# Row maxima subtracted once in four key steps, convolution weights loaded late, and GpSimd's product behind the additions

## The chip, the cores and the metric

The kernel runs on one core of a Trainium2 chip. The metric is the device time of one execution in microseconds. A core has five engines that matter here: TensorE (PE; its weight loads are shown apart as PEld), VectorE (DVE), ScalarE (ACT), GpSimd (POOL) and SyncE (SP), which only issues DMAs. Each works through its own list of instructions in order, and waits for the others by semaphores. TensorE writes to PSUM; the other data lie in SBUF.

## What is computed

Two layers, one behind the other, on an input of 2 x 256 x 64 x 64 in float32, so 4096 positions with 256 channels for each of two batches. The first is self-attention with 8 heads of 32 channels, the second a non-local block with 2x2 max pooling. Cut to what matters:

```python
# layer 0, for each batch b and head h; i, j run over 4096 positions
q, k, v = split(w_qkv @ x)
scores = einsum('bhdi,bhdj->bhij', q, k) / sqrt(32)
attn = softmax(scores, axis=-1)
out = einsum('bhij,bhdj->bhdi', attn, v)
x1 = w_proj @ out + x

# layer 1
g_x = maxpool2(conv1x1(x1, g_w, g_b))
theta_x = conv1x1(x1[:, :64], theta_w, theta_b)
phi_x = maxpool2(conv1x1(x1[:, 64:], phi_w, phi_b))
y = softmax(theta_x^T @ phi_x, axis=-1) @ g_x
return batchnorm(conv1x1(y, W_w, W_b)) + x1
```

The softmax subtracts the exact maximum of every row before the exponential, so the maxima of all 4096 x 4096 scores of each head are found first.

## The kernel before

**Quads and blocks.** Four heads are worked on together, one on each group of 32 partitions; that is a quad. Two batches of two quads make four, numbered n = 0 to 3. A quad's 4096 queries come in 8 blocks of 512 (index i), so there are 32 blocks, numbered here 0 to 31 in order of time; the first batch has blocks 0 to 15, the last quad has blocks 24 to 31. A block goes through its keys in 32 steps of 128 keys (index j).

**One step.** `attend` (from L376) issues a step so: `subtract` writes minus the row maxima into a PSUM tile of two banks, one for each head of a pair of heads (L413, a matmul of ones with rows that hold each maximum as a sum of three bfloat16 terms); `score` adds the scores (L401); ACT takes the exponential (L537) into p. A quad is two such pairs, with two tiles. While this goes on, `weigh` for the step before multiplies the exponentials by v (L425), and VectorE adds the result to num (L436).

**Differences of keys.** The subtraction isn't done in every step. An even step subtracts and then adds the scores with its keys. An odd step goes on with the same tile: its keys are taken 512 positions further on, and what is added to the tile are the scores with the differences of the keys of two chunks of 512 (kd for the first half of the positions, last_kd for the second). So the tile holds the odd step's scores less the maxima, with no subtraction. GpSimd makes these differences (L214 in the first quad, `differences` at L229 later).

**Maxima, one block ahead.** In each step, twice, `advance(maxes)` puts in a piece of the search for the next block's maxima: two products of 128 queries with 512 keys each time (L252), on the two groups of 32 rows that the scores beside them don't use. VectorE reduces them, either plainly (L264) or as a pair of chunks: ACT keeps the positive part of the product with a key difference (L271), and VectorE adds the other product and takes the maximum in one instruction (L278). The first block of a new quad has fewer pairs and more plain maxima. At the end of a block's maxima, near step 28, `negate` (L133) splits them in three bfloat16 terms on GpSimd, in one of two tiles by turns, and `make_rows` turns them by four small matmuls (L147) into the rows that `subtract` uses.

**Sums of exponentials.** The denominators are built in part by GpSimd: for two heads it adds each step's p to a running sum (L455), and for the other two it issues a DMA that adds two steps' p to one of two sums (L463, 1 MB each). p comes from rings: 6 buffers for the first kind and 5 double ones for the second, and a buffer is free when its addition or its DMA has ended.

**Normalization** (`normalize`, L465) runs inside the next block. A last accumulating DMA joins the two sums (L469), matmuls make den (L481), ACT copies it to r (L489). SP stores one row of each head and loads it back spread over 128 partitions (L498, L499), VectorE takes the reciprocals there (L503), SP stores them and loads them back broadcast (L504, and four loads at L506), and GpSimd multiplies num by r into y (L511). In the built order L511 stands behind the addition of step 13; nothing in the source ties it there.

**Projections for the blocks to come.** `during` (L233) lists for each block what is made of x: in six of eight blocks, k and v of the next quad together behind step 15, and q of this quad two blocks on behind step 27; in the last two, three items behind steps 11, 19 and 27. `make` (L165) loads x through SP into the single buffer of the pool xs, unless the same part of x is still held there, and does the matmuls (L183, L195). In the last quad there is no next quad, so only q is left.

**Around it.** A prologue of about 103 us makes the first quad's q, k, v and the first maxima. After a batch's 16 blocks, `project` (L557) adds the projected output to x, and `non_local` (L581) does the second layer. The weights of both (wproj, theta, phi) lie in SBUF for the whole run; ACT's queue loads them at the start.

Of the kernel before, what the change touches and what calls it, by code (L numbers as in the profile page):

```python
# [9 lines left out]
F32 = mybir.dt.float32  # L10
BF16 = mybir.dt.bfloat16
# [5 lines left out]
N = HH * WW  # L17
# [18 lines left out]
def conv_attention(  # L36
# [45 lines left out]

    wqk_sb = const.tile([P, NC, QUADS, 2, P], F32, name="wqk_sb")
    wv_sb = const.tile([P, NC, C], F32, name="wv_sb")
    wproj_sb = const.tile([P, NC, C], F32, name="wproj_sb")
    theta_w = const.tile([CM, 2 * CM], F32, name="theta_w")
    phi_w = const.tile([P, NC, 2 * CM], F32, name="phi_w")
    par = const.tile([P, NPAR], F32, name="par")

    def load_x(b, i, t):  # L90
# [7 lines left out]
    nc.scalar.dma_start(out=wproj_sb, in_=wproj.rearrange("(o p) m -> p o m", p=P))  # L98
    nc.scalar.dma_start(out=theta_w, in_=thetaw)
    nc.scalar.dma_start(out=par, in_=params)  # L100

    nc.scalar.dma_start(out=phi_w[CM:P, 0, :], in_=phiw[0 : P - CM, :])
    nc.scalar.dma_start(out=phi_w[:, 1, :], in_=phiw[P - CM :, :])

    ident = work.tile([P, P], F32, tag="r", name="ident", bufs=1)
    make_identity(nc, ident)
# [19 lines left out]

    terms = [const.tile([P, NB // P, QH, D], BF16, name=f"terms_{i}") for i in range(2)]
    for t in terms:  # L130
        nc.gpsimd.memset(t, 0.0)

    def negate(name, n, neg):  # L133


        t = terms[n % 2]
# [28 lines left out]
    def make(what, n, i):  # L165
        b, qd = QUAD[n]
        if (b, i) not in held:
            name = f"x_{what}_{n}_{i}"
            if attending:
                held.clear()  # L170
                to = xs.tile([P, NC, NB], F32, tag="x", name=name)
            else:
                to = single(name)
            held[b, i] = load_x(b, i, to)
        xc = held[b, i]
        name = f"{what}_{b}_{qd}_{i}"
        pq = scratch(name)
        if what == "v":
            if i == 0:
                v[n] = qkv.tile([P, NJ, QH, D], F32, tag="v", name=f"v_{n}")  # L180
            for j in range(NB // P):
                for c in range(NC):
                    nc.tensor.matmul(  # L183
                        pq[:, bass.ts(j, P)],
                        xc[:, c, bass.ts(j, P)],
                        wv_sb[:, c, bass.ts(qd, P)],
                        start=(c == 0),
                        stop=(c == NC - 1),
                    )
                if j % 2 == 1:  # L190
                    yield
            nc.scalar.copy(v[n][:, bass.ts(i, NB // P)].rearrange("p j h d -> p (j h d)"), pq)
            return
        for c in range(NC):
            nc.tensor.matmul(  # L195
                pq,
                wqk_sb[:, c, qd, 0 if what == "q" else 1, :],
                xc[:, c, :],
                start=(c == 0),
                stop=(c == NC - 1),  # L200
            )
            yield
        if what == "q":
            to = q[n, i] = qkv.tile([P, NB], F32, tag="q", name=f"q_{n}_{i}", bufs=3)
        else:
            if i == 0:
                k[n] = qkv.tile([P, N], F32, tag="k", name=f"k_{n}")
            to = k[n][:, bass.ts(i, NB)]
        nc.scalar.copy(to, pq)
        if what == "k" and i % 2 == 1 and n == 0:  # L210
            if i == 1:
                kd[n] = qkv.tile([P, NI // 4, NB], F32, tag="kd", name=f"kd_{n}")
            two = k[n][:, bass.ts(i // 2, 2 * NB)]
# [15 lines left out]
        nc.gpsimd.tensor_sub(to, two[:, :, 1, :], two[:, :, 0, :])  # L229

    def during(n, i):  # L233
        if i < NI - 2:
            return [[("k", n + 1, i), ("v", n + 1, i)], [("q", n, i + 2)]]
        if i == NI - 2:
            return [[("k", n + 1, i)], [("k", n + 1, i + 1)], [("q", n + 1, 0)]]
        return [[("v", n + 1, i - 1)], [("v", n + 1, i)], [("q", n + 1, 1)]]


    reduced, cut = None, None
# [92 lines left out]
    def maxima(n, i):  # L334
        if (n, i) == (0, 0):
            yield from first_block()
        else:
            heads = [of_head(n, i, h) for h in range(QH)]
            for step in range(G * NI):

                for two in ((2, 3) if step % 2 == 0 else (3, 2)), (0, 1):
                    for h in two:
                        next(heads[h])
                    yield
        neg = work.tile([P, NB // P, QH], F32, tag="neg", name=f"neg_{n}_{i}")
        nc.vector.tensor_reduce(neg, part, AX.X, ALU.max, negate=True)
        rows.append(negate(f"{n}_{i}", len(rows), neg))
        if i == 0 and n > 0:
            nc.vector.memset(part[:, :, 2:, :], LEAST)

# [10 lines left out]
    def advance(steps, n=1):  # L361
        for _ in range(n):
            next(steps, None)
# [12 lines left out]
    def attend(b, y):  # L376
# [10 lines left out]

        def keys(j):


            return j // 8 * 8 + j % 2 * 4 + j % 8 // 2

        def score(s, pair, blk, j):

            if j % 2:
                kj = (last_kd if j >= NJ // 2 else kd[blk.n])[:, j // 8 % 2, bass.ts(j % 8 // 2, P)]
            else:
                kj = k[blk.n][:, bass.ts(keys(j), P)]
            for t in range(2):
                h = 2 * pair + t  # L400
                nc.tensor.matmul(  # L401
                    s[:, t, :],
                    kj[bass.ts(h, D), :],
                    q[blk.n, blk.i][bass.ts(h, D), :],
                    start=False,
                    stop=True,
                    skip_group_check=j % 2 == 1,
                )

        def subtract(s, pair, blk):  # L410
# [54 lines left out]
        def normalize(blk):  # L465
# [27 lines left out]
            else:  # L493
# [14 lines left out]
                    )  # L508
                for _ in range(13):
                    yield  # L510
            nc.gpsimd.tensor_mul(y[:, blk.qd, bass.ts(blk.i, NB)], blk.num, r)  # L511

        waiting, normal = None, iter(())
        for qd in range(QUADS):
            for i in range(NI):
                blk = Block(qd, i)
                groups = during(blk.n, i)
                items = [[x for x in g if x[1] < len(QUAD)] for g in groups]
# [38 lines left out]
    def project(b, y, normal):  # L557
        for i in range(NI):
            if i == NI // 2:
                for _ in normal:  # L560
# [17 lines left out]
        return ap.rearrange("p (r a w b) -> p r w a b", a=2, w=WW // 2, b=2)  # L578


    def non_local(b, y):  # L581
# [76 lines left out]
        def maxima1():  # L658
            for i in range(NI):
# [17 lines left out]
                ready.append(negate(f"l1_{b}_{i}", i, neg))  # L677
                yield

        maxes1 = maxima1()  # L680
# [100 lines left out]
    attending = True  # L781
    for b in range(B):
        y = big.tile([P, NC, N], F32, tag="y", name=f"y{b}")
        project(b, y, attend(b, y))
        non_local(b, y)


_OUT = (B, C, HH, WW)
# [51 lines left out]
```

## Time and profile before

Three runs took 4070.07 to 4077.61 us, median 4073.38.

| | us |
|---|---|
| median of three runs | 4073.38 |
| the profiled execution, its own time | 4072.18 |
| its span, from the first instruction to the last | 4070.4 |
| prologue | 0 to 103 |
| attention, batch 0, blocks 0 to 15 | 103 to 1809 |
| projection and second layer, batch 0 | 1809 to 2100 |
| attention, batch 1, blocks 16 to 31 | 2100 to 3777 |
| projection and second layer, batch 1 | 3777 to 4070 |

The attention is 3383 of the 4070 us. How busy each engine is there shows in the view by windows. Its columns are the stretch, its length, and for each engine its busy time and number of instructions, then the granted clock, DMA's share and GB/s:

```profile
103.00:954.00 851.00, 849.73 (x6972) 316.45 (x6968) 678.92 (x1284) 635.62 (x790) 688.60 (x408) 1.00 0.77 160
2952.00:3777.00 825.00, 812.12 (x6542) 280.39 (x6539) 625.15 (x1159) 617.66 (x754) 650.19 (x390) 0.99 0.77 161
```

The order is PE, PEld, VectorE, ACT, POOL. The first line is quad 0, the second quad 3, which makes no k and v. In both PE is busy almost throughout, at the full clock, and VectorE, ACT and POOL for 75 to 81% of the time.

A matmul of float32 operands is recorded as two matmuls. That is why L425, with four matmuls in a step, shows as a group of 8. The subtraction's operands are bfloat16, and there the record is one.

### The profile page before, as it was taken

What the parts mean: (1) busy time and instruction counts of PE and PEld (TensorE: products, weight loads), DVE (VectorE), ACT (ScalarE), POOL (GpSimd) and SP (SyncE); (2) the same over time, 40 slices, a digit from 0 to 9 for tenths busy, and PEclk for the clock granted to TensorE, in tenths of its full rate; (3) what the DMA queues carried; (4) which work ended last, traced back from release to release, by engine and by line L of the source; (5) the groups of instructions that cost most, each with busy time, mean ns of one, the idle gap of its engine ahead of it and who ended that gap; (6) DMA issues with size and microseconds to landing.
All of it is one profiled execution on the core that took longest, in us unless ns stands there. A gap on an engine that the chain in (4) does not pass through costs nothing.

```text
span 4070.4 us, 75211 instructions
## 1 busy us (share of the span) xinstructions
PE 4021.6 (99%) x29616; PEld 1495.2 (37%) x29616; DVE 2974.8 (73%) x5451; ACT 2673.8 (66%) x3329; POOL 2892.5 (71%) x1844
## 2 busy tenths in 40 slices
PE   9999999999999999999999999999999999999998
PEld 4333333333333333333333333333333333332333
DVE  5877877788778777774457777777888888784444
ACT  5777777777777777751147777777677777776111
POOL 0888887778778888761457888787888888776143
PEclk9999999999999999999999999999999999999999
DMA  1677777777777777780027777778777777778200
GB/s 59 143 161 161 155 164 160 159 162 164 156 161 163 165 161 160 165 197 0 25 51 159 161 161 162 165 160 173 161 165 161 158 155 164 154 151 173 76 16 26
DMA packets 113380, 569.35 MB, mean 140 GB/s; under 512 B 20232, under 2 KB 22024, under 8 KB 51840
## 3 DMA queue, kind: packets, MB, share of 16 engines
q0 software_dynamic: 68832, 501.25, 60.5%
q1 hardware_dynamic: 42928, 62.10, 5.0%
q8 instruction: 232, 3.80, 0.4%
q10 hardware_dynamic: 1264, 1.19, 0.1%
q14 instruction: 124, 1.02, 0.1%
HBM read 54.39 MB, written 8.88 MB: 16 GB/s over the span
## 4 chain that ended last, share of the span: by engine, by line
PE 89%; DMA 5%; DVE 2%; POOL 1%; issue 1%; ACT 1%; SPq 0%; POOLq 0%; DVEq 0%; ACTq 0%
PE ps L252 27%; PE w L425 23%; PE s L401 17%; PE y L698 5%; PE s L413 5%; DMA p<-p 3%; DMA flat<-few 2%; PE q L195 2%; PE den L481 1%; PE k L195 1%; PE proj L567 1%; PE g L623 1%; PE v L183 1%; DVE r L712 1%; PE f L666 1%
## 5 line engine op out<-in xcount | busy, mean ns | idle before, releaser
L455 POOL TENSOR_TENSOR p<-p,p 128x1024 f32<-128x1024 f32 x945 | 2331.0, 2467 | 444.5 <-ACT p L537 308.1
L252 PE MATMUL ps<-k,q 32*128 32x512 f32 x6232 | 2116.6, 618 | 2.4 <-DVE part L278 1.0
L537 ACT ACTIVATE p<-s 128x1024 f32<-128x1024 f32 x2048 | 1987.3, 1026 | 134.2 <-PE ps L252 46.1
L264 DVE TENSOR_REDUCE part<-ps 128x1 f32<-128x512 f32 x2136 | 1372.6, 686 | 138.2 <-PE s L401 66.4
L425 PE MATMUL w<-p,v 128*32 128x512 f32 x8192 | 1093.4, 605 | 0.0
L278 DVE CUSTOM_DVE_ANT_0 ps<-ps,over 128x512 f32<-128x512 f32 x980 | 683.8, 700 | 540.3 <-PE ps L252 299.1
L401 PE MATMUL s<-q,k 32*128 32x512 f32 x4096 | 1038.0, 594 | 0.0
L271 ACT ACTIVATE over<-ps 128x512 f32<-128x512 f32 x916 | 546.9, 597 | 578.2 <-PE ps L252 533.9
L252 PEld LDWEIGHTS ps<-k,q 32*128 32x128 f32 x6232 | 788.8, 184 | 261.6 <-DVE num L436 75.4
L436 DVE TENSOR_TENSOR num<-num,w 128x512 f32<-128x512 f32 x992 | 671.7, 677 | 42.3 <-PE w L425 39.4
L252 PE MATMUL ps<-kd,q 32*128 32x512 f32 x1056 | 568.4, 643 | 1.0 <-POOL kd L214 0.7
L401 PE MATMUL s<-q,last_kd 32*128 32x512 f32 x2048 | 515.2, 616 | 12.1 <-ACT p L537 12.1
L401 PE MATMUL s<-q,kd 32*128 32x512 f32 x2048 | 513.1, 617 | 2.0 <-ACT p L537 2.0
L252 PE MATMUL ps<-last_kd,q 32*128 32x512 f32 x904 | 482.1, 640 | 1.5 <-POOL last_kd L214 1.5
L425 PEld LDWEIGHTS w<-p,v 128*32 128x32 f32 x8192 | 161.5, 108 | 778.9 <-ACT over L271 689.4
L463 POOL DMA_DIRECT2D p<-p x448 | 388.4, 867 | 70.7 <-ACT p L537 67.4
L413 PE MATMUL s<-rows,ones_b 32*128 32x512 bf16 x2048 | 394.5, 381 | 0.1
L401 PEld LDWEIGHTS s<-q,k 32*128 32x128 f32 x4096 | 371.3, 184 | 10.6 <-issue 7.2
L413 PEld LDWEIGHTS <-ones_b 32*128 32x128 bf16 x2048 | 132.6, 91 | 504.4 <-PE ps L252 251.6
L401 PEld LDWEIGHTS s<-q,last_kd 32*128 32x128 f32 x2048 | 172.5, 184 | 232.4 <-ACT p L537 219.9
L401 PEld LDWEIGHTS s<-q,kd 32*128 32x128 f32 x2048 | 174.8, 185 | 224.4 <-ACT p L537 196.8
L698 PE MATMUL y<-p,kv 128*128 128x512 f32 x512 | 240.0, 608 | 6.4 <-DVE r L712 6.4
(106 smaller groups left out, 2239.7 us busy)
## 6 DMA issues: line engine op xcount, KB each, us to landing
p<-p POOLq DMA_DIRECT2D x478, 1024.0 KB, 7.6
x_k<-in_x_dram SPq DMA_DIRECT2D x32, 512.0 KB
x_q<-in_x_dram SPq DMA_DIRECT2D x30, 512.0 KB
x_res<-in_x_dram SPq DMA_DIRECT2D x16, 512.0 KB
out_dram<-z SPq DMA_DIRECT2D x16, 512.0 KB
r<-flat SPq DMA_DIRECT2D x120, 64.0 KB
x_v<-in_x_dram SPq DMA_DIRECT2D x6, 512.0 KB
wqk_sb<-in_wqk_dram ACTq DMA_DIRECT2D x1, 512.0 KB
```

Source lines behind the costliest of these rows:

```text
L252: nc.tensor.matmul(ps, q[n, i][bass.ts(h, D), bass.ts(g, P)], keys[bass.ts(h, D), :], start=True, stop=True,)
L264: reduced = nc.vector.tensor_reduce(part[:, g, h, j : j + 1], ps, AX.X, ALU.max)
L271: cut = nc.scalar.activation(over, ps, AF.Relu)
L278: reduced = nc.vector.tensor_tensor_reduce(out=ps, in0=ps, in1=over, scale=1.0, scalar=LEAST, op0=ALU.add, op1=ALU.max, accum_out=part[:, ...
L401: nc.tensor.matmul(s[:, t, :], kj[bass.ts(h, D), :], q[blk.n, blk.i][bass.ts(h, D), :], start=False, stop=True, skip_group_check=j % 2 == 1,)
L413: nc.tensor.matmul(s[:, t, :], ones_b[bass.ts(h, D), :], rows[blk.rows][bass.ts(h, D), :], start=True, stop=False,)
L425: nc.tensor.matmul(w[bass.ts(h, D), :], v[blk.n][:, keys(j), h, :], p[h // 2][:, h % 2, :], start=True, stop=True,)
L436: nc.vector.tensor_add(blk.num, blk.num, w)
L455: added = nc.gpsimd.tensor_add(blk.sums[0], blk.sums[0], p[0])
L463: nc.gpsimd.dma_start(out=blk.sums[n], in_=two, accum_op=ALU.add)
L537: nc.scalar.activation(p[pair], s, AF.Exp, scale=scale)
L698: nc.tensor.matmul(acc[i][o], wg[:, 2 * t + j, bass.ts(o, P)], p[:, j, :], **edge)
```

## The change

**Keys in fours.** A half of the positions (2048) has four chunks of 512. Steps now go through them in fours: the first with the keys of chunk 0, the next with kd (chunk 1 less chunk 0), then with a new tile mid_kd (chunk 2 less chunk 1), then with the second part of kd or last_kd (chunk 3 less chunk 2). `subtract` is called, and a tile taken, in one step of four instead of one of two. mid_kd is a constant tile of two halves that GpSimd fills in the new function `between`: in the prologue for the first quad, later in step 18 of the block before a quad (first half) and in step 2 of a quad's first block (second half).

**Weights.** The three weights leave the constant tiles. `late_weights` takes the buffer of x at the end of a batch's attention and loads them there by four DMAs of SP, once for each batch.

**One tile of terms** instead of two.

**Order of the projections.** All blocks now have up to three items behind steps 11, 19 and 27: q first, then k, then v, where k and v were together before.

**The product with the reciprocals** is issued behind `added`, the last addition that stands before it in the source. In the built order that is step 25's addition.

Two effects show in the built order of SP: the load of x for k stands before the store of the reciprocals (L504) in most blocks, and the weights' loads stand before those of x_res. The instructions of VectorE are the same, in the same order.

```diff
-    wproj_sb = const.tile([P, NC, C], F32, name="wproj_sb")
-    theta_w = const.tile([CM, 2 * CM], F32, name="theta_w")
-    phi_w = const.tile([P, NC, 2 * CM], F32, name="phi_w")
...
+    def late_weights(b):
+
+        t = xs.tile([P, NC, NB], F32, tag="x", name=f"weights_{b}")
+        project_w = t[:, 0, :].rearrange("p (c m) -> p c m", c=NC)
+        phi_w = t[:, 1, :C].rearrange("p (c m) -> p c m", c=NC)
+        theta_w = t[:CM, 1, C : C + 2 * CM]
+        nc.sync.dma_start(out=project_w, in_=wproj.rearrange("(o p) m -> p o m", p=P))
+        nc.sync.dma_start(out=theta_w, in_=thetaw)
+
+        nc.sync.dma_start(out=phi_w[CM:P, 0, :], in_=phiw[0 : P - CM, :])
+        nc.sync.dma_start(out=phi_w[:, 1, :], in_=phiw[P - CM :, :])
+        return project_w, theta_w, phi_w
...
-    terms = [const.tile([P, NB // P, QH, D], BF16, name=f"terms_{i}") for i in range(2)]
-    for t in terms:
-        nc.gpsimd.memset(t, 0.0)
...
+    t = const.tile([P, NB // P, QH, D], BF16, name="terms")
+    nc.gpsimd.memset(t, 0.0)
...
+        if what == "k" and i % 4 == 2 and n == 0:
+            between(n, i // 4)
...
+    mid_kd = const.tile([P, 2, NB], F32, name="mid_kd")
+
+    def between(n, half):
+        two = k[n][:, N // 2 * half + NB :]
+        nc.gpsimd.tensor_sub(mid_kd[:, half, :], two[:, NB : 2 * NB], two[:, :NB])
...
         if i < NI - 2:
-            return [[("k", n + 1, i), ("v", n + 1, i)], [("q", n, i + 2)]]
+            return [("q", n, i + 2), ("k", n + 1, i), ("v", n + 1, i)]
...
-            return j // 8 * 8 + j % 2 * 4 + j % 8 // 2
+            return j // 16 * 16 + j % 4 * 4 + j % 16 // 4
 
         def score(s, pair, blk, j):
 
-            if j % 2:
-                kj = (last_kd if j >= NJ // 2 else kd[blk.n])[:, j // 8 % 2, bass.ts(j % 8 // 2, P)]
+            half, c, cols = j // 16, j % 4, bass.ts(j % 16 // 4, P)
+            if c == 0:
+                kj = k[blk.n][:, bass.ts(keys(j), P)]
+            elif c == 2:
+                kj = mid_kd[:, half, cols]
             else:
-                kj = k[blk.n][:, bass.ts(keys(j), P)]
+                kj = (last_kd if half else kd[blk.n])[:, c // 2, cols]
...
-            nc.gpsimd.tensor_mul(y[:, blk.qd, bass.ts(blk.i, NB)], blk.num, r)
+            with tc.issue_after(added.ins):
+                nc.gpsimd.tensor_mul(y[:, blk.qd, bass.ts(blk.i, NB)], blk.num, r)
...
-                        if j % 2 == 0:
+                        if j % 4 == 0:
                             s = both[pair] = scores(f"s_{blk.name}_{j}_{pair}")
                             subtract(s, pair, blk)
                             advance(maxes)
...
+                        if (i, j) == (0, 2) and blk.n > 0:
+                            between(blk.n, 1)
                         if (i, j) == (0, NJ // 4) and blk.n > 0:
                             differences(blk.n, 1, last_kd)
-                    elif items and j in ((15, 27), (11, 19, 27))[len(groups) - 2]:
-                        for item in items.pop(0):
-                            advance(make(*item), 9)
+                        if (i, j) == (NI - 1, NJ // 2 + 2) and blk.n + 1 < len(QUAD):
+                            between(blk.n + 1, 0)
+                    elif j % 8 == 3 and j > 8 and items:
+                        advance(make(*items.pop(0)), 9)
```

More of the change, by code (lines that the diff above doesn't have):

```diff
@@ L97, in conv_attention @@
     nc.scalar.dma_start(out=wv_sb, in_=wv.rearrange("(o p) m -> p o m", p=P))
-    nc.scalar.dma_start(out=wproj_sb, in_=wproj.rearrange("(o p) m -> p o m", p=P))
-    nc.scalar.dma_start(out=theta_w, in_=thetaw)
     nc.scalar.dma_start(out=par, in_=params)
-    nc.scalar.dma_start(out=phi_w[CM:P, 0, :], in_=phiw[0 : P - CM, :])
-    nc.scalar.dma_start(out=phi_w[:, 1, :], in_=phiw[P - CM :, :])
+    def late_weights(b):
[8 more added lines that the diff above has]
+        return project_w, theta_w, phi_w
     ident = work.tile([P, P], F32, tag="r", name="ident", bufs=1)
@@ L124, in conv_attention, with negate @@
     nc.vector.tensor_add(bn_shift, bn_shift, par[:, BETA : BETA + NC])
-    terms = [const.tile([P, NB // P, QH, D], BF16, name=f"terms_{i}") for i in range(2)]
-    for t in terms:
-        nc.gpsimd.memset(t, 0.0)
-    def negate(name, n, neg):
-        t = terms[n % 2]
+    t = const.tile([P, NB // P, QH, D], BF16, name="terms")
+    nc.gpsimd.memset(t, 0.0)
+    def negate(name, neg):
         rest = work.tile([P, NB // P, QH], F32, tag="rest", name=f"rest_{name}")
@@ L229, in differences @@
         nc.gpsimd.tensor_sub(to, two[:, :, 1, :], two[:, :, 0, :])
+    mid_kd = const.tile([P, 2, NB], F32, name="mid_kd")
+    def between(n, half):
+        two = k[n][:, N // 2 * half + NB :]
+        nc.gpsimd.tensor_sub(mid_kd[:, half, :], two[:, NB : 2 * NB], two[:, :NB])
     def during(n, i):
         if i < NI - 2:
-            return [[("k", n + 1, i), ("v", n + 1, i)], [("q", n, i + 2)]]
+            return [("q", n, i + 2), ("k", n + 1, i), ("v", n + 1, i)]
         if i == NI - 2:
-            return [[("k", n + 1, i)], [("k", n + 1, i + 1)], [("q", n + 1, 0)]]
-        return [[("v", n + 1, i - 1)], [("v", n + 1, i)], [("q", n + 1, 1)]]
+            return [("k", n + 1, i), ("k", n + 1, i + 1), ("q", n + 1, 0)]
+        return [("v", n + 1, i - 1), ("v", n + 1, i), ("q", n + 1, 1)]
     reduced, cut = None, None
@@ L346, in maxima @@
         nc.vector.tensor_reduce(neg, part, AX.X, ALU.max, negate=True)
-        rows.append(negate(f"{n}_{i}", len(rows), neg))
+        rows.append(negate(f"{n}_{i}", neg))
         if i == 0 and n > 0:
@@ L406, in score @@
                     stop=True,
-                    skip_group_check=j % 2 == 1,
+                    skip_group_check=j % 4 > 0,
                 )
@@ L516, in attend @@
                 blk = Block(qd, i)
-                groups = during(blk.n, i)
-                items = [[x for x in g if x[1] < len(QUAD)] for g in groups]
+                items = [x for x in during(blk.n, i) if x[1] < len(QUAD)]
                 both = [None, None]
@@ L547, in attend, with project @@
                         make_rows()
+                        if (i, j) == (0, 2) and blk.n > 0:
+                            between(blk.n, 1)
                         if (i, j) == (0, NJ // 4) and blk.n > 0:
                             differences(blk.n, 1, last_kd)
-                    elif items and j in ((15, 27), (11, 19, 27))[len(groups) - 2]:
-                        for item in items.pop(0):
-                            advance(make(*item), 9)
+                        if (i, j) == (NI - 1, NJ // 2 + 2) and blk.n + 1 < len(QUAD):
+                            between(blk.n + 1, 0)
+                    elif j % 8 == 3 and j > 8 and items:
+                        advance(make(*items.pop(0)), 9)
         weigh(*waiting)
         return normalize(blk)
-    def project(b, y, normal):
+    def project(b, y, normal, wproj_sb):
         for i in range(NI):
@@ L578, in pooled, with non_local @@
         return ap.rearrange("p (r a w b) -> p r w a b", a=2, w=WW // 2, b=2)
-    def non_local(b, y):
+    def non_local(b, y, theta_w, phi_w):
         theta = [double(f"theta_{b}_{t}") for t in range(2)]
@@ L676, in maxima1 @@
                 nc.vector.tensor_copy(neg[:, :, 2], neg[:, :, 0])
-                ready.append(negate(f"l1_{b}_{i}", i, neg))
+                ready.append(negate(f"l1_{b}_{i}", neg))
                 yield
@@ L783, in conv_attention @@
         y = big.tile([P, NC, N], F32, tag="y", name=f"y{b}")
-        project(b, y, attend(b, y))
-        non_local(b, y)
+        normal = attend(b, y)
+        project_w, *conv_w = late_weights(b)
+        project(b, y, normal, project_w)
+        non_local(b, y, *conv_w)
 _OUT = (B, C, HH, WW)
```

## The prediction, made before the changed kernel ran

> **What bounds it now.** I read the page first: the busy row, the chain, and the groups of the attention loop.
>
> ```profile
> span 4070.4 us, 75211 instructions
> PE 4021.6 (99%) x29616; PEld 1495.2 (37%) x29616; DVE 2974.8 (73%) x5451; ACT 2673.8 (66%) x3329; POOL 2892.5 (71%) x1844
> ...
> PE 89%; DMA 5%; DVE 2%; POOL 1%; issue 1%; ACT 1%; SPq 0%; POOLq 0%; DVEq 0%; ACTq 0%
> ...
> L455 POOL TENSOR_TENSOR p<-p,p 128x1024 f32<-128x1024 f32 x945 | 2331.0, 2467 | 444.5 <-ACT p L537 308.1
> ...
> L413 PE MATMUL s<-rows,ones_b 32*128 32x512 bf16 x2048 | 394.5, 381 | 0.1
> ```
>
> PE is busy nearly all the time and carries 89% of the chain, so work taken off PE counts. But neither row prices a matmul. Those with 32 rows run beside each other, so the 394.5 us of L413 are mostly other matmuls' time too. The price is in the timeline of PE alone: L425 closes each step j of a block, and the distance between its groups is the length of a step. Four in a row (columns: start, length, line, operation, count):
>
> ```profile
> 1008.86 1.07 PE L425 MATMUL w<-p,v 128*32 128x512 f32 x8
> 1011.85 1.06 PE L425 MATMUL w<-p,v 128*32 128x512 f32 x8
> 1014.98 1.07 PE L425 MATMUL w<-p,v 128*32 128x512 f32 x8
> 1017.97 1.06 PE L425 MATMUL w<-p,v 128*32 128x512 f32 x8
> ```
>
> The intervals are 2.99, 3.13, 2.99 us. The 3.13 ones hold an even step, with the four L413 matmuls; the 2.99 ones hold an odd step, which adds a difference of keys to the scores that are there. Over all blocks, leaving out the steps in which a projection or a denominator is put in, the medians are 3.134 us (288 intervals) and 2.991 us (256). A regular block takes 106.53 us, time after time; almost nothing but PE varies it.
>
> The exception is in the view of the waits (total, times, longest), and in POOL's and ACT's timelines around one such place:
>
> ```profile
> POOL y L511 <- DMA r<-flat: 138.5, 25, 8.0
> ACT p L537 <- DMA p<-p: 25.9, 21, 3.2
> ```
>
> ```profile
> 575.91 1.27 POOL L511 TENSOR_TENSOR y<-num,r 128x512 f32<-128x512 f32 x1 [6.67 <-DMA r<-flat]
> 577.12 0.86 POOL L463 DMA_DIRECT2D p<-p  x1
> 577.72 5.09 POOL L455 TENSOR_TENSOR p<-p,p 128x1024 f32<-128x1024 f32 x2
> 582.76 0.87 POOL L463 DMA_DIRECT2D p<-p  x1
> ```
>
> ```profile
> 587.52 1.02 ACT L537 ACTIVATE p<-s 128x1024 f32<-128x1024 f32 x1 [1.79 <-DMA p<-p]
> ```
>
> POOL stands 6.67 us at L511 for the reciprocals, issues its accumulating DMA late, that DMA returns its buffer late, and an exponential, then PE, waits for the buffer. Behind such a wait POOL needs 5.64 us for two steps (577.12 to 582.76) and PE 6.12, so it catches up 0.24 us a step; the k and v projections give it another 3.7 us. In the last quad (from 2952 us) there is no k or v to make, and there most blocks stall.
>
> **Half of the subtractions.** Of 2048 L413 matmuls 1024 go: 8 of 16 even steps in each of 32 blocks take the odd step's form. In the built order these steps hold the same PE instructions as an odd step, in the same order. So 3.134 - 2.991 = 0.143 us for each. Of 256, 9 lie in stretches of blocks 7, 15 and 23 where every step already takes 3.1 to 3.3 us, even or odd: the next quad's first maxima are plain, VectorE sets the pace, and the gain is hidden. Another 8 lie in the very last block, where no maxima run: there the steps alternate between 2.37 us with subtraction and 3.04 without, since the odd one waits for the exponentials. I take a gain of 1 us for these 8: at best 8 x 0.22 = 2, the time by which their subtraction delays the scores; at worst a loss of 8 x 0.67 = 5, if each takes the 3.04. So 239 x 0.143 = 34, plus 1: **35 us**.
>
> This is where a rule and the trace part. The Trainium skill (TensorE: Matmul & The Clock Gate, Back-to-back issue gap) has about 216 ns for a warm one-pass matmul of 512 columns. A step's subtractions are two pairs, each pair in two row groups at once: 2 x 216 = 0.43 us, and 256 x 0.43 = 110 us. The trace shows 0.143, because products on the other two row groups run beside each pair. The measured difference decides; 110 is the far end.
>
> What is next late in three odd-type steps in a row? VectorE: one joint maximum (0.70 + 0.14), two plain (1.29 for both), one addition (0.68): 2.81 us. POOL: 5.64 / 2 = 2.82. ACT: 0.60 + 1.94 = 2.54. All under 2.99, VectorE and POOL barely. If one of them held the middle steps at 3.13, the 35 us would be 0.
>
> **The product with the reciprocals.** L511 moves on POOL from behind the addition of step 13 to that of step 25, some 36 us later, when the four loads of r have long landed: in the example they end at 575.8, around step 15. So 30 waits of 4.4 to 8 us leave POOL's queue; its 1.27 us stays. What is worth anything on PE is the stall behind them. Summing what intervals near steps 15 to 23 exceed their median, I get 16 us (12 of them in the last quad), and 3 us in the last block: **19 us**, against the 25.9 us that ACT waited in all, some of it hidden by PE's queue. Queued behind L511 at its new place are the DMA of step 24's pair, two additions and the five small operations of negate. Their result is read by L147: in block 15 negate ends at 1796.7 and L147 starts at 1804.4, 7.7 us to spare for 1.27. The buffers num and r are next written in a later block.
>
> **The order of the projections.** q comes at step 11, k at 19, v at 27, one by one, for k and v together at 15 and q at 27. Together k and v cost 6.83 - 3.13 = 3.70 us; alone, in blocks 6 and 7, 1.92 and 1.98. So 0.20 us more in 18 blocks: **-3 us**. Here a rule speaks against the change: waits of a DMA are held by the sequencer that issues it (DMA: Bandwidth & Descriptors, Anatomy of one DMA), so a queue is blocked by its first waiting entry. On SP the load of x for k now stands before the store of the reciprocals (L504), and it waits for q's last matmul. By the trace that matmul falls before step 12's scores, while the reciprocal (564.22) is ready in step 13: the load goes first anyway, cost 0; by the rule alone, at most a step, 3 us, which r now has to spare. A load has 8 steps (24 us) to land; loads at that distance in blocks 6 and 7 show no excess.
>
> **The rest.** mid_kd adds 8 subtractions of 128x512 on POOL, 1.26 us each by those of L214: two in the prologue, where POOL is nearly idle, six in steps 2 and 18 of blocks in which POOL catches up 0.2 us a step; 0, at most 6 x 1.3 = 8 us if it had no slack. The weights read late are four DMAs on SP behind the last x, issued at about 1795 (x_res follows at 1798.5), 14 us before the projection (1809.4); wqk, twice as large as the projection's weights, took 5.23 us to land. Cost 0, or up to 6 us twice if the slack is gone. Four DMAs and one table load less at the start, but k's copy now stands behind the square root, which waits for par: 0, give or take 1.5. One terms buffer: its next writer comes a block later (in the second layer after several more PE matmuls), 0.
>
> **Sum.** 35 + 19 - 3 = 51 us. The profiled execution took 4072.2 us (span 4070.4), 1.2 below the median 4073.4 of the runs shown; 4072.2 - 51 = **4021 us**.
>
> **Rivals.**
> - Only PE's part comes: POOL, with its additions, mid_kd and L511, is late elsewhere and the 19 us return. For: POOL's pace is within 7% of PE's. Against: 5 us of waiting leave each block. 4072 - 35 + 3 = 4040.
> - The middle steps are held by VectorE or POOL: 4072 - 19 + 3 = 4056. For: 2.81 and 2.82 of 2.99, and blocks 7, 15, 23. Against: odd steps already run at 2.99.
> - The subtractions cost PE their full 0.43: 4072 - 110 - 19 + 3 = 3946. Against: the measured intervals.
> - Slower: r comes after its new place, and POOL waits there with negate behind it. PE then waits at L147 for what exceeds 7.7 - 1.3 = 6.4 us, in 30 blocks; with 9 us of wait 30 x 2.6 = 78, so 4099. It decides from 6.4 + 51/30 = 8.1 us of wait; for it speaks only the load put before L504, against it some 34 us of margin.
>
> **How the numbers follow.** Sum as worked out: 0.66, 4010 to 4032. PE's part alone 0.13; stalls alone 0.07; full price or part of it 0.06; both gains lost (about 4072) 0.05; slower 0.03. The range 4003 to 4046 takes in the whole of the second case (4040) and the open ends of mid_kd and the start (8 and 1.5 us); below, it goes as far as a quarter of the distance to the full price (75 / 4 = 18). The stalls alone, most of the full price, the lost gains and the slower case stay outside: about 0.2. What a measurement of this kernel can tell from no change is about 0.2%, 8 us: faster 0.92, same 0.05, slower 0.03.
>
> **What would show it.** L413 at 1024; in three of four steps 2.99 us between groups of L425, and 3.13 in the fourth; a regular block near 105.6 us; no wait of POOL at the product for r, and ACT's wait for p's DMA near 6 us. It is wrong if middle steps take 3.1 (VectorE or POOL next), if ACT still waits over 15 us for that DMA, or if L147 waits for terms.

## The result, and the profile after

The changed kernel took 4027.68 us in the median of 4 runs (4026.04 to 4027.83), the kernel before 4072.91 in the 4 beside it: a ratio of 0.9889, 95% interval 0.9875 to 0.9904. The profiled execution took 4027.58 us, at a clock of 0.997. Its span is 44.9 us shorter than the span before; 51 were forecast. The time is near the forecast, but the profile shows that its terms were not.

The page of the kernel after, with the rows that answer to those shown of before:

```profile
span 4025.5 us, 72980 instructions
...
PE 3993.3 (99%) x28592; PEld 1460.0 (36%) x28592; DVE 2959.7 (74%) x5451; ACT 2668.1 (66%) x3328; POOL 2898.1 (72%) x1851
...
PE 97%; DVE 2%; ACT 0%; POOL 0%; DMA 0%; issue 0%; DVEq 0%; ACTq 0%
...
L469 POOL TENSOR_TENSOR p<-p,p 128x1024 f32<-128x1024 f32 x945 | 2293.6, 2427 | 569.9 <-ACT p L551 442.6
```

PE has 1024 fewer matmuls: half of the subtractions (now L427) are gone. PE carries 97% of the chain where it carried 89%, and the 5% of DMA have left it. POOL stood 444.5 us before its additions and now stands 569.9, mostly for ACT's exponentials. So POOL has more slack than before, and no longer sets when a buffer comes free.

The view of the waits, for the two that the forecast wanted gone (total, times, longest):

```profile
POOL y L526 <- DVE r L506: 41.6, 2, 21.6
ACT p L551 <- DMA p<-p: 2.3, 5, 0.8
```

The 25 waits of POOL for the loads of r are gone, and with them five more that the view of before puts down to VectorE (26.4 us); two waits for VectorE's reciprocals are left, where no next block follows and the product has no later place. ACT waits 2.3 us for p's DMA, where it waited 25.9.

The timeline of PE, four ends of steps in a row (start, length, line, operation, count):

```profile
491.58 1.06 PE L439 MATMUL w<-p,v 128*32 128x512 f32 x8
494.71 1.07 PE L439 MATMUL w<-p,v 128*32 128x512 f32 x8
497.70 1.06 PE L439 MATMUL w<-p,v 128*32 128x512 f32 x8
500.79 1.07 PE L439 MATMUL w<-p,v 128*32 128x512 f32 x8
```

The intervals are 3.13 (a step with subtraction), 2.99 (the odd step after it) and 3.09 (the middle step, which has lost its subtraction). The forecast wanted 2.99 in the middle step. It got shorter by 0.04 us, not by 0.143.

### The profile page after: what moved, and what is told of

It reads as the page before. It is cut to its first block, busy times and chain, and to the rows that moved or that the text cites. A ratio compares the mean times of both kernels' runs of the same rounds, so it can differ in the third digit from the quotient of the medians.

```text
span 4025.5 us, 72980 instructions
## 1 busy us (share of the span) xinstructions
PE 3993.3 (99%) x28592; PEld 1460.0 (36%) x28592; DVE 2959.7 (74%) x5451; ACT 2668.1 (66%) x3328; POOL 2898.1 (72%) x1851
## 4 chain that ended last, share of the span: by engine, by line
PE 97%; DVE 2%; ACT 0%; POOL 0%; DMA 0%; issue 0%; DVEq 0%; ACTq 0%
PE ps L264 27%; PE w L439 25%; PE s L415 24%; PE y L715 5%; PE s L427 3%; PE v L186 2%; PE q L198 2%; PE k L198 2%; PE den L495 1%; PE proj L584 1%; PE g L640 1%; DVE r L729 1%; PE f L683 1%; PE f L749 1%; PE tp L624 0%; PE tp L620 0%
## 5 line engine op out<-in xcount | busy, mean ns | idle before, releaser
L469 POOL TENSOR_TENSOR p<-p,p 128x1024 f32<-128x1024 f32 x945 | 2293.6, 2427 | 569.9 <-ACT p L551 442.6
L264 PE MATMUL ps<-k,q 32*128 32x512 f32 x6232 | 2115.5, 619 | 2.4 <-DVE part L290 1.0
L551 ACT ACTIVATE p<-s 128x1024 f32<-128x1024 f32 x2048 | 1983.4, 1024 | 106.5 <-PE ps L264 61.2
L264 PEld LDWEIGHTS ps<-k,q 32*128 32x128 f32 x6232 | 809.7, 184 | 207.6 <-DVE part L276 48.6
L450 DVE TENSOR_TENSOR num<-num,w 128x512 f32<-128x512 f32 x992 | 670.7, 676 | 38.5 <-PE w L439 34.4
L264 PE MATMUL ps<-kd,q 32*128 32x512 f32 x1056 | 568.4, 643 | 1.0 <-POOL kd L219 0.7
L415 PE MATMUL s<-q,k 32*128 32x512 f32 x2048 | 514.6, 593 | 0.0
L415 PE MATMUL s<-q,mid_kd 32*128 32x512 f32 x2048 | 509.6, 615 | 0.0
L264 PE MATMUL ps<-last_kd,q 32*128 32x512 f32 x904 | 481.1, 639 | 1.5 <-POOL last_kd L219 1.5
L415 PEld LDWEIGHTS s<-q,mid_kd 32*128 32x128 f32 x2048 | 173.5, 183 | 309.3 <-ACT p L551 306.8
L764 ACT ACTIVATE p<-f 128x1024 f32<-128x1024 f32 x64 | 65.5, 1024 | 248.5 <-PE f L749 219.2
```

The costliest lines, as they stand in the source:

```text
L264: nc.tensor.matmul(ps, q[n, i][bass.ts(h, D), bass.ts(g, P)], keys[bass.ts(h, D), :], start=True, stop=True,)
L415: nc.tensor.matmul(s[:, t, :], kj[bass.ts(h, D), :], q[blk.n, blk.i][bass.ts(h, D), :], start=False, stop=True, skip_group_check=j % 4 > 0,)
L450: nc.vector.tensor_add(blk.num, blk.num, w)
L469: added = nc.gpsimd.tensor_add(blk.sums[0], blk.sums[0], p[0])
L551: nc.scalar.activation(p[pair], s, AF.Exp, scale=scale)
```

## The experiments

In the sessions below the kernel before had medians of 4070.1 to 4073.8, each on a chip of its own. So a difference of a few us between kernels of two sessions is read only where the intervals between steps show it too.

### The parts one by one

**e1: subtraction in every second step again**, all else as changed.

```diff
-            return j // 16 * 16 + j % 4 * 4 + j % 16 // 4
+            return j // 8 * 8 + j % 2 * 4 + j % 8 // 2
...
-                        if j % 4 == 0:
+                        if j % 2 == 0:
```

> The changed kernel with the subtraction in every second step again (keys in twos, mid_kd never filled); late weights, order of projections and L511's new place stay. The prediction's price (0.143 us for each removed step's subtraction, 35 us in all): about 4062. Theory after the first look at the trace of after (a middle step takes 3.09, not 2.99, so a subtraction is worth only 0.04 us): steps of 3.13 and 2.99 by turns again, about 12 us more than the changed kernel, 4040.

It took 4036.34 us (4035.51 to 4037.13), 0.9915 of before (0.9901 to 0.993). That is 8.7 us above the changed kernel, so half of the subtractions were worth 9 us, not 35. The steps were 3.13 and 2.99 by turns again.

**e2: the product with the reciprocals back at its old place**, all else as changed.

```diff
-            with tc.issue_after(added.ins):
-                nc.gpsimd.tensor_mul(y[:, blk.qd, bass.ts(blk.i, NB)], blk.num, r)
+            nc.gpsimd.tensor_mul(y[:, blk.qd, bass.ts(blk.i, NB)], blk.num, r)
```

> The changed kernel with the product with the reciprocals at its old place on GpSimd, behind step 13's addition. If that place is worth what the prediction put on it, whatever else stands around it: about 19 us more, 4046. If the wait is caught up by whatever is projected next behind it, it now costs more, since k no longer comes at step 15 but only at 19: then nearly every block stalls near step 17 as the last quad's blocks did before, 30 x 1.7 us and the last block's 7: about 4080, with GpSimd waiting 4 to 8 us at the product in every block and ACT waiting for p's DMA over 40 us.

**e3: the product moved, and nothing else** changed from the kernel before.

```diff
-            nc.gpsimd.tensor_mul(y[:, blk.qd, bass.ts(blk.i, NB)], blk.num, r)
+            with tc.issue_after(added.ins):
+                nc.gpsimd.tensor_mul(y[:, blk.qd, bass.ts(blk.i, NB)], blk.num, r)
```

> The kernel before, with only the product with the reciprocals moved behind step 25's addition. Theory: all stalls go and nothing else does: 18 us less, about 4054; steps of 3.13 and 2.99 by turns; 6.83 at step 15 with k and v, 5.79 at step 27 with q. Rival: the stalls were late additions that come at another place, no change.

e3 took 4046.25 us (4045.22 to 4048.84), 0.9941 (0.9925 to 0.9958): 24 us less than before. Its view of the waits:

```profile
POOL y L512 <- DVE r L492: 42.8, 2, 21.6
...
ACT p L538 <- DMA p<-p: 1.0, 2, 0.5
```

The one line by itself takes away the waits for the loads of r and nearly all of ACT's waiting. Six blocks of the last quad, 103.40 to 107.35 us each before, became 102.83 or 102.84.

e2 took 4066.79 us (20 runs, 4061.35 to 4075.43), 0.999 (0.9983 to 0.9997): 39 us above the changed kernel, more than e3 gained. Its waits show where the rest comes from:

```profile
POOL y L525 <- DMA r<-flat: 148.1, 27, 10.4
...
ACT p L550 <- DMA p<-p: 33.3, 24, 3.4
```

These are more than the 138.5 and 25.9 of before, and the time lies between the two that were expected. The interval that begins with the w of step 17 has a median of 3.65 us, where it had 2.99. Before, k and v stood at step 15 and gave POOL 3.7 us to catch up before the late buffer was wanted; in the new order nothing stands there. So the parts of the change depend on each other: the new order of the projections pays only with the product out of the way. That k's place is the cause fits these intervals, but no run moved k alone.

**e4: k, v and q at steps 11, 19 and 27**, all else as changed.

```diff
-            return [("q", n, i + 2), ("k", n + 1, i), ("v", n + 1, i)]
+            return [("k", n + 1, i), ("v", n + 1, i), ("q", n, i + 2)]
```

> The changed kernel with q behind step 27 and k and v behind 11 and 19, one by one, in the six blocks concerned of the first three quads (q alone at 11 in the last quad, as changed). The prediction's reason (k and v apart cost 0.2 us more than together, the place of q costs nothing): no change, 4028. Theory from the trace of after: it is q that costs 0.67 us more at step 27 than v does, since the first products of the next maxima wait for ACT's copy of that q: 18 x 0.67 = 12 us more, 4040, with 5.79 us at step 27.

It took 4039.62 us (4038.67 to 4039.77), 0.9923 (0.9908 to 0.9938): 11.9 above the changed kernel. So the place of q counts. The timeline of the kernel before, with q behind step 27 (the part in brackets is idle time and what ended it):

```profile
400.62 1.98 PE L195 MATMUL q<-x_q,wqk_sb 128*128 128x512 f32 x4
402.54 0.39 PE L413 MATMUL s<-rows,ones_b 32*128 32x512 bf16 x2
402.64 0.59 ACT L209 COPY q<-q 128x512 f32<-128x512 f32 x1 [1.84 <-PE q L195]
...
403.28 0.18 PEld L252 LDWEIGHTS ps<-kd,q 32*128 32x128 f32 x1 [0.33 <-ACT q L209]
```

And the kernel after, with v there:

```profile
398.88 2.05 PE L186 MATMUL v<-wv_sb,x_k 128*128 128x128 f32 x16
400.86 0.39 PE L427 MATMUL s<-rows,ones_b 32*128 32x512 bf16 x2
...
400.86 0.18 PEld L264 LDWEIGHTS ps<-kd,q 32*128 32x128 f32 x1
```

Behind step 27 the maxima of the block after next begin, and their products need the q that was just made. PE must wait until ACT has copied it: L252 starts 0.74 us after the first subtraction (403.28 - 402.54). Behind v, L264 starts together with the subtraction. The interval is 5.79 us with q and 5.12 with v, and e4 has 5.79 in all blocks of the first three quads. 18 blocks changed their last item, which makes 18 x 0.67 = 12.1; v at step 19 takes 5.12 where k took 5.05, 1.3 more. 11.9 was measured. The weight loads' waits for that copy, before and after:

```profile
PEld ps L252 <- ACT q L209: 9.8, 30, 0.3
PEld ps L264 <- ACT q L212: 2.0, 6, 0.3
```

There were 30 of them before, one for each q behind step 27, and 6 after; e4 has 24, and the next run none.

**e11: q first in the last two blocks of a quad too**, where the changed kernel still had it behind step 27 (there two items of k or v come first, not q).

```diff
-            return [("k", n + 1, i), ("k", n + 1, i + 1), ("q", n + 1, 0)]
-        return [("v", n + 1, i - 1), ("v", n + 1, i), ("q", n + 1, 1)]
+            return [("q", n + 1, 0), ("k", n + 1, i), ("k", n + 1, i + 1)]
+        return [("q", n + 1, 1), ("v", n + 1, i - 1), ("v", n + 1, i)]
```

> The changed kernel with q first in the last two blocks of a quad as well. Theory of the copy: step 27's interval falls from 5.79 to 5.12 in 6 more blocks: 4 us less, 4024. Rival: in these blocks it is the pair of items around it that costs, no change.

It took 4022.81 us (4021.81 to 4023.07), 0.9876 (0.9862 to 0.9891). The two ratios' intervals overlap, so the 4.9 us below the changed kernel rest on the trace: the six intervals of 5.79 became 5.05 and 5.12, which gives 4.2, and the span is 4.6 shorter. Of the kernels that leave nothing out it is the shortest.

### Why the middle step keeps its length

PE's own order in a middle step is that of an odd step, yet the step is 0.10 longer. VectorE is 74% busy and not saturated. The timeline shows what differs. First an odd step (it begins at 495.71):

```profile
495.71 0.19 PEld L415 LDWEIGHTS s<-q,last_kd 32*128 32x128 f32 x2 [0.84 <-ACT p L551]
...
495.92 0.68 DVE L450 TENSOR_TENSOR num<-num,w 128x512 f32<-128x512 f32 x1
...
496.65 0.21 PEld L264 LDWEIGHTS ps<-k,q 32*128 32x128 f32 x2 [0.20 <-DVE num L450]
```

Then the middle step behind it (it begins at 498.70):

```profile
498.70 0.19 PEld L415 LDWEIGHTS s<-q,mid_kd 32*128 32x128 f32 x2 [0.84 <-ACT p L551]
...
499.01 0.68 DVE L450 TENSOR_TENSOR num<-num,w 128x512 f32<-128x512 f32 x1
...
499.74 0.29 PEld L264 LDWEIGHTS ps<-k,q 32*128 32x128 f32 x2
```

The products of the maxima and w share a ring of four PSUM buffers, and a step takes five. So the last product of a step (L264) needs the buffer of w, which VectorE returns when its addition to num (L450) has ended: at 496.60 (495.92 + 0.68) and 499.69 (499.01 + 0.68), and the weight load comes 0.05 us behind it in both. In the odd step VectorE begins the addition 0.21 us into the step, in the middle step 0.31. So the product comes 0.94 us into the odd step and 1.04 into the middle one, and the step ends 0.10 later. A step with subtraction gives VectorE time to catch up; behind an odd step it has none. This chain was read from the trace. The next runs test it by making VectorE's work smaller.

**e5: plain maxima over half of the columns.** **e6: the same, with subtraction in every second step** as in e1. **e9: plain maxima over 448 of 512 columns.** All three leave keys out of the search for the maxima, so they show what VectorE costs and are no faster versions. The edit of e5 in VectorE's reduction of a plain product, where e9 has `NB // 8 * 7` in place of `NB // 2`:

```diff
-        reduced = nc.vector.tensor_reduce(part[:, g, h, j : j + 1], ps, AX.X, ALU.max)
+        reduced = nc.vector.tensor_reduce(part[:, g, h, j : j + 1], ps[:, : NB // 2], AX.X, ALU.max)
```

> The changed kernel, in which VectorE's plain maxima read only 256 of the 512 columns of each product (so the maxima leave out half of these keys); PE, ACT and GpSimd do the same work. Some 0.27 us less for each plain maximum, 0.54 a step. Theory: a middle step is held at 3.09 by VectorE, whose addition to num gives back late the PSUM buffer that the step's last product needs; with VectorE early, middle steps take 2.99 like the others, and about 7 x 31 x 0.10 = 22 us go, 4006. Rival: 3.09 is PE's own time (in even steps the maxima's pair product comes from the other head): middle steps stay at 3.09 and the time changes by less than 8 us.

> The same halved maxima with the subtraction in every second step (the first experiment's kernel). Theory: without VectorE in the way the subtraction has the price that the prediction read from odd and even steps: 0.14 us each, so about 35 us over the run with halved maxima and keys in fours, near 4040. Rival: its price is 0.04 us with or without VectorE: 12 us over that run.

> The changed kernel, in which the plain maxima read 448 of 512 columns (an eighth of these keys is left out of the maxima): 0.067 us less for each, 0.13 a step. If a middle step waits for VectorE by 0.10 us and an odd one by 0.06, as the run with half the columns says (2.93 for both), an eighth is already enough: middle steps 2.93 to 2.99, and 50 to 75 us go, 3953 to 3978. If the gain of that run came in proportion to VectorE's work: a quarter of 75 us, 19, so 4009.

e5 took 3952.83 us (3952.82 to 3952.85), 0.9709 (0.9681 to 0.9738): 75 below the changed kernel. Nothing of PE, ACT, POOL or the DMAs was taken away, and the clock was the same (0.998 to 0.997); the reduction's mean went from 686 to 420 ns:

```profile
L276 DVE TENSOR_REDUCE part<-ps 128x1 f32<-128x512 f32 x2136 | 1373.7, 686 | 87.9 <-PE ps L264 57.7
L276 DVE TENSOR_REDUCE part<-ps 128x1 f32<-128x256 f32 x2136 | 810.4, 420 | 136.2 <-PE ps L264 100.4
```

Four of its steps, on PE:

```profile
580.37 1.07 PE L439 MATMUL w<-p,v 128*32 128x512 f32 x8
583.30 1.06 PE L439 MATMUL w<-p,v 128*32 128x512 f32 x8
586.23 1.07 PE L439 MATMUL w<-p,v 128*32 128x512 f32 x8
589.36 1.06 PE L439 MATMUL w<-p,v 128*32 128x512 f32 x8
```

And four of e6:

```profile
584.95 1.06 PE L434 MATMUL w<-p,v 128*32 128x512 f32 x8
587.88 1.06 PE L434 MATMUL w<-p,v 128*32 128x512 f32 x8
591.01 1.06 PE L434 MATMUL w<-p,v 128*32 128x512 f32 x8
593.94 1.07 PE L434 MATMUL w<-p,v 128*32 128x512 f32 x8
```

In e5 the steps without subtraction take 2.93 us, odd and middle alike; the one with it still takes 3.13. In e6 3.13 and 2.93 take turns. So the odd steps too were held by VectorE, at 2.99; my theory had counted the middle steps alone, which is why 22 us were expected and 75 came. e6 took 3998.43 us (3996.75 to 4000.11), 0.9821 (0.9793 to 0.985): 45.6 above e5 for 256 subtraction steps, 0.18 us each. That is what a step's subtractions cost when VectorE is not late, and no less than the 0.143 forecast; with VectorE late only 0.04 of it can be had in a middle step.

e9 took 3981.18 us (3980.66 to 3981.69), 0.9775 (0.9755 to 0.9794): 46 below the changed kernel and 3 above the range expected, with odd steps at 2.93 and middle ones at 3.02. A quarter of e5's cut (an eighth of the columns instead of a half) gives 62% of its gain.

The traces of the three kernels show why, in steps 15 to 27 of blocks 1 to 30, without 16 and 20. In each step the weight load stands about 0.05 us behind the end of VectorE's addition. And the length of a step without subtraction goes with the time at which the addition begins, counted from the first matmul of w (medians):

| steps | addition begins, us | step, us |
|---|---|---|
| changed kernel, middle | 1.31 | 3.09 |
| e9, middle | 1.24 | 3.02 |
| changed kernel, odd | 1.20 to 1.21 | 2.99 |
| e9, odd | 1.13 | 2.93 |
| e5, odd and middle | 1.13 | 2.93 |

The matmuls of w take 1.07 us. So at 1.13 VectorE begins as soon as w is there, and a faster reduction has nothing left to give; e9 has come so far in its odd steps, e5 in all.

**e7: each remaining subtraction issued twice**, the second over the first.

```diff
-            for t in range(2):
+            for turn in range(2):
+                for t in range(2):
...
-                    stop=False,
+                        stop=turn == 0,
```

> The changed kernel with each remaining subtraction issued twice (four more one-pass matmuls of 512 columns in one step of four, 1024 in all). If PE pays for them what even and odd steps differed by: 256 x 0.14 = 36 us more, 4064. If nothing runs beside them[...]: 256 x 0.43 = 110 us more, 4138. If PE has slack in these steps too: under 12 us.

It took 4076.76 us (18 runs, 4075.51 to 4078.1), 1.0014 (1.0007 to 1.0022): 49 above the changed kernel, which is none of the three expectations, but nearest to the first. The steps with subtraction went from 3.13 to 3.36, 0.23 us for four more matmuls; the others of a regular block stayed within 0.03. So the row groups do run beside each other: adding four costs far less than the 0.43 of the isolated gap, and about six times what removing four had gained.

### Two tries at a faster version

If VectorE is the delay, ACT could take part of the maxima. **e8** makes two chunks of the maxima of heads 0 and 1 as a pair, as heads 2 and 3 do; **e10** does so for head 0 alone, with four bfloat16 buffers for ACT's part in place of two in float32.

```diff
-        chunks = 0 if h < 2 else NI // 2 if i == 0 and n > 0 else NI
+        chunks = 2 if h < 2 else NI // 2 if i == 0 and n > 0 else NI
```

```diff
-        over = work.tile([P, NB], F32, tag="over", name=f"over_{n}_{i}_{g}_{h}")
+        over = work.tile([P, NB], BF16, tag="over", name=f"over_{n}_{i}_{g}_{h}", bufs=4)
...
-        chunks = 0 if h < 2 else NI // 2 if i == 0 and n > 0 else NI
+        chunks = 2 if h == 0 else 0 if h == 1 else NI // 2 if i == 0 and n > 0 else NI
```

> The changed kernel with two of eight chunks of heads 0 and 1 handled as a pair too (8 pairs a block): for each pair VectorE does 0.84 us instead of 1.29, ACT 0.60 more. Theory, if VectorE holds the middle steps: the steps concerned get shorter, 2 of 8 middle steps in a block to 2.99, 6 us in all. Rival: ACT, at 2.54 us a step, has 3.14 there and becomes the bound: 8 steps a block 0.1 to 0.3 us longer, 30 to 70 us more.

> The changed kernel with two of eight chunks of head 0 alone handled as a pair, and four buffers of over in bfloat16 in the place of two in float32 (so that the maxima found differ in their last bits). Theory: without the wait for a buffer of over, VectorE has 0.55 us less to do in 8 steps of a block and 0.10 more in 8; up to 4 middle steps a block lose their 0.10 to 0.16, 12 to 20 us less, 4008 to 4016. Rival: ACT's 0.60 more comes between the two exponentials of a step, and the scores of the next wait for the second: 0.3 us in 4 steps a block, 35 us more, 4063.

e8 took 4470.34 us (4469.22 to 4471.46), 1.0981 (1.0949 to 1.1012): 443 above the changed kernel, and neither expectation. Its waits have a new row:

```profile
ACT over L283 <- DVE part L290: 257.6, 126, 3.7
```

ACT now waits for VectorE to return its two buffers, four times a block, and the exponentials stand behind it. Around the end of a block eight steps, from 29 to 4 of the next, take 4.1 to 5.2 us in place of 3.0 to 3.3. As the trace has it, the relief was overrun by a new loop; no run gave e8 more buffers alone, so that is read and not tested. e10 took 4040.23 us (4039.89 to 4041.34), 0.992 (0.9904 to 0.9937), 12.6 above the changed kernel, and again neither expectation: the first interval of a block fell from 3.27 to 3.15, but near the end, where the next pairs begin, one rose from 3.25 to 3.56, and ACT's added work delays the exponentials (the weight loads of the scores wait 794.3 us for them instead of 735.0). Which of the two outweighs in another split was not tried.

## Why the forecast was right, and where it was not

Four profiled spans lead from one kernel to the other: before 4070.4, the product moved (e3) 4044.3, all but the subtractions and mid_kd (e1) 4033.3, all 4025.5. The steps between them are the terms of the sum:

| term | forecast us | measured us |
|---|---|---|
| the product with the reciprocals | -19 | -26.1 |
| order of the projections, and the rest | +3 | -11.0 |
| half of the subtractions | -35 | -7.8 |
| sum | -51 | -44.9 |

Each span is of one execution, and the kernel before varied by 11 us in one session (4065.96 to 4077.34). The medians of the runs give 23.9, 9.9 and 8.7 for the three terms, so their order of size stands.

The forecast came within 6 us of the span's change by luck: 27 us too many for the subtractions stand against 7 and 14 too few for the other two.

**The subtractions: the step that failed.** "In the built order these steps hold the same PE instructions as an odd step, in the same order. So 3.134 - 2.991 = 0.143 us for each." The premise holds and the conclusion doesn't. The difference of two neighbours was taken as a price; but the odd step was at 2.99 only because the longer step before it had let VectorE catch up, as e5 shows by bringing odd and middle steps to the same 2.93. A sign of it stood in the waits of before:

```profile
PEld ps L252 <- DVE num L436: 75.4, 400, 0.2
```

Of these 400 weight loads 307 lie in odd steps: the step that served as the measure was itself waiting for VectorE. The rival with VectorE or POOL in the middle steps, given 0.07, was the right mechanism for this part. Its ground, VectorE's 2.81 us of work in a step of 2.99, could not decide it: the busy time fits, and the delay is in a loop of PSUM buffers through both engines. POOL's work is the same in e5, so POOL didn't hold these steps.

**The rule and the row.** The Trainium skill's section (TensorE: Matmul & The Clock Gate, Back-to-back issue gap) was weighed with its isolated gap, 0.43 us for a step's two pairs. The section itself says that this gap counts too much at large N, and gives 131 ns per matmul for a sustained stream, which makes an estimate of 0.26 us for the two pairs. Measured with VectorE relieved: 0.18 to 0.20; doubled: 0.23. So the stream's figure is the nearer to the price on PE, and neither tells what a removal gains here.

**The product with the reciprocals: right, its size too small.** The wait went as described, and no new wait came at the new place. Between e3 and before, blocks 0 to 30 lost 16.8 us (16 forecast) and the last block 9.8 (3 forecast). The term mis-sized is the last block: I had counted its stall in the interval behind the w of step 13 (5.97 to 2.48 us), but not the stall at its denominator, behind the w of step 5 (8.62 to 4.07). The waits at the denominators for p's DMA, 5.3 us in all before (3.1 of the weight loads, 2.2 of PE), are 0.2 in e3.

**The projections: wrong sign.** "So 0.20 us more in 18 blocks" priced k and v apart, and put the move of q from step 27 to step 11 at nothing. In a regular block the four intervals in question were 6.83 + 5.79 + 3.13 + 3.13 = 18.88 us and are 3.13 + 5.12 + 5.05 + 5.05 = 18.35. Taking k and v apart costs 1.92 + 1.99 - 3.70 = 0.21, as forecast. But q costs 2.66 us behind step 27 (5.79 - 3.13) and 1.92 behind step 11, 0.74 less; 18 x 0.53 = 9.5. Who needs the result at once was not asked of q. In the last quad nothing takes its place at step 27, the interval there still has 3.76 us, and a block gains only 0.12 by the move (102.83 in e3, 102.71 in e1). The load of x for k in front of the store of the reciprocals cost nothing that shows: POOL has no wait for the loads of r left.

**The rest: right.** From the last w of block 15 to the first of block 16, where the late weights are loaded and the second layer runs, 293.3 us passed both before and after. Block 7, in which GpSimd fills the first half of mid_kd, took 108.57 us before and 108.64 after. The first steps of the attention began 0.3 us later. Two small slips in the working have no weight: 18 x 0.20 is 3.6 us, not 3, and 5.64 of 6.12 us leaves POOL 8%, not 7.

Of the signs named, L413 at 1024, POOL's wait came as said, and ACT's, with 2.3 us, better than said. The middle steps at 3.09 were the sign of being wrong. The block of 105.6 came too (105.65), but for another reason: 0.53 us from the projections and 0.35 from the steps, instead of 8 x 0.143 = 1.14 less 0.20. A total that fits doesn't show that its terms do.

## What to carry to other kernels

The difference between a step with an instruction and a step without it is its price only if the shorter step would be as short beside another short one; look in the trace for a buffer that another engine returns in the middle of the step, and compare its time relative to the step's start. Before a producer is moved, or left where it is, ask who needs its result next: work that stands directly in front of its own reader exposes the copy between them. A wait in the queue of an engine that is not the bound is worth moving behind that engine's other work when, as here, one of its DMAs returns a buffer to the engine that is.

## What the runs showed of the hardware

An engine that is 74% busy held the steps of another that was 99% busy: cutting its reduction from 686 to 420 ns took 75 us off a kernel from which PE had lost nothing, and a cut to 620 ns already 46. The sign of it in the profile before was a row of weight loads that waited up to 0.2 us for VectorE, 400 times.

Four small bfloat16 matmuls in a step had four prices: 0.04 us removed from the middle steps, 0.143 as the difference of neighbours, 0.18 to 0.20 with VectorE relieved, and 0.23 added a second time.
